# Layer 0 of a four-layer graph network: a prebuilt mark list, a last evaluation that only counts, shorter candidate lists, and a tie removal behind a branch

## The chip, the cores and the metric

The kernel runs on one NeuronCore of a Trainium2 chip. The core has five engines that run their own instruction streams in order and wait for each other through semaphores: TensorE (PE: matrix products and transposes into PSUM), VectorE (DVE), ScalarE (ACT), GpSimd (POOL, which here starts the indirect gathers) and SyncE (SP, which here starts nearly all other transfers). The metric is the time of one execution in microseconds (us) on the device. The kernel before took 3152.24 us (median of 3 runs, 3150.27 to 3155.07).

## The reference

The input is x (4096 nodes, 256 features) and adj (4096 x 4096, about one entry in a thousand nonzero, and a full diagonal). Four layers follow each other, each as `x = x + layer(relu(layernorm(x)), adj)`. Only layer 0 matters here:

```python
def _top_p_attention(X, W1, W2, W3):
    q = X @ W1.T @ W2.T
    k = X @ W3.T
    probs = softmax(q @ k.T / TAU)
    idx = jnp.argsort(-probs, axis=-1)
    sp = jnp.take_along_axis(probs, idx, axis=-1)
    cs = jnp.cumsum(sp, axis=-1)
    keep_sorted = cs - sp < TOP_P                     # TOP_P = 0.9
    mask = zeros(probs.shape, bool).at[rows, idx].set(keep_sorted)
    A = probs * mask
    return A / jnp.maximum(A.sum(-1, keepdims=True), 1e-12)

R = S + eye(N); R = R / R.sum(-1, keepdims=True)      # S is adj
Z = 0; Xf = X; Xa = X
for n in range(2):
    A = _top_p_attention(Xa, W1, W2, W3)
    Xf = R @ Xf
    Xa = A @ Xa
    Z = Z + Xf @ U1[n].T + Xa @ U2[n].T
h = X + Z
return layernorm(h) * ln_g + ln_b
```

So each of two steps needs, in every row of a 4096 x 4096 matrix of probabilities, the smallest set of largest entries whose sum reaches 0.9, and the product of that cut matrix with a 4096 x 256 one. No sort is needed: a threshold per row is enough, if it is the exact one and ties at it are treated as the sort treats them.

## The kernel before, in words

Rows are worked on in 32 blocks of 128. `layer0_step(n, ...)` builds step n. It is a software pipeline: one call of `period(b, ...)` issues parts of several blocks, in an order that is written out as text in `ORDERS[n]` (L1096). A word such as `take4@-1` calls `take`, group 4, for block b-1; `s1@2` calls the Sign evaluation 1 for block b+2. The order of the words is the order of the instructions on VectorE, ScalarE and TensorE, for these three are under a manual schedule; so a word that waits holds up all words behind it that use the same engine. `fill` words are places where a given number of steps of some other generator is issued (`period`, L1820, with the numbers in the loops near the end of the file).

What happens to one block, in order of time:

- `logits0/1` (L1139) multiply queries and keys on TensorE, `exps0/1` (L1158) take exponentials on ScalarE into the tile `e` (128 x 4096).
- Four evaluations look for a threshold. Words `s0 r0 s1 r1 s2 r2 s3 r3` are `evaluate` (L1170): with Sign, ScalarE counts the entries over the current guess, with Relu it sums what lies under it. 0 and 1 read 1024 columns, 2 and 3 all 4096. After evaluations 0, 1, 2 small 128 x 1 steps on VectorE (`measured`, `update`, `stepped`) make the next guess; the words are `first`, `second` (`second_short` in step 1) and `third`. After evaluation 3, `bound` (L1255) makes an upper end `hi` with a margin over the guess (constant `AHEAD`).
- `below` (L1328) takes the entries under `hi` into `near` (L1331, all 4096 columns); `maxima`, `some_maxima` list the eight largest of each of 16 segments (L1339); `order` merges them into a descending list of `LIST` = 48 per row, eight by eight (`listing`, L1350 MAX8 and L1353 MATCH_REPLACE8).
- `decide` (L1358) finds the exact threshold and the number of tied entries to leave out (`extra`); `cut` (L1401) zeroes everything under the threshold.
- `drop` removes the tied entries with one `match_replace` over 4096 columns (L1413). In step 0 it stands behind a branch: `ties_pe` (TensorE) sums `extra` over the rows, `ties` (ScalarE) casts that to an integer, and `tc.If` skips the removal where it is zero. In step 1 it always runs.
- `flip` g transposes four of the 32 128 x 128 pieces of `e` (TensorE, L1469), `take` g copies them to SBUF (ScalarE, L1475), `attend` g multiplies them with the node features (TensorE, L1484), g from 0 to 7; `attended` scales by the row sum's inverse (L1493).

Step 0 then does per block `turn` and `turned` (transposes), `keys` for step 1, and the products with U1 and U2: `xa_pe` and `h_pe` (`weighted`, L1519). `copy_xa` (ScalarE, L1542) copies one half of the result and `store_xa` (VectorE, L1546) adds the node's own features to the other half; `store_h` (L1536) copies the second product. Step 0 also marks where adj is nonzero: `load_adj` loads the 512 KB quarters of a block's rows, and eight `mark` words per period (L1498, 128 x 512 to 128 x 4 each) take the maxima of absolute values on VectorE. After step 0, `listed_columns` turns the marks into lists of columns (MAX8 and MATCH_REPLACE8 over 1024 columns, L794).

Step 1 uses the lists: `reach` (L1568) gathers the needed rows of adj and of node features with indirect transfers on POOL (`gather`, L835: 20 per period in the first half of the blocks, 10 gathers per block of nodes), and `mix` (L1581, products L850) forms R @ Xf from them. `mix0` and `mix1` work on two blocks per period; the first 16 periods make the first product, the second 16 the second one, and in the second half also the sum with the heads (`add_heads`, L1615), the layer norm (`spread`, `finish`, `level`, `normalised`) and the projection of layer 1. `verify` (L1444) tests in every row that the lists were long enough; if one was not, the whole layer is done again by a general and slow path (L2259).

Layers 1 to 3 follow and are not touched.

Of the kernel before, what the change touches and what calls it, by code (L numbers as in the profile page):

```python
# [63 lines left out]
F32 = mybir.dt.float32  # L64
# [6 lines left out]
ALU = mybir.AluOpType  # L71
# [5 lines left out]
P = 128  # L77
# [16 lines left out]
LIST = 48  # L94
AHEAD = 16.0
# [3 lines left out]
QUARTERS = 4  # L99
CHUNKS = 5  # L100
# [554 lines left out]
def fast_layers(  # L655
# [82 lines left out]
    def load_adj(pool, ib):  # L738

        parts = []  # L740
        for c in range(0, NB, CA):
            t = pool.tile([P, CA, P], F32, name="adj", tag="adj")
            nc.sync.dma_start(t, adjt[ib, :, c : c + CA, :])
            parts.append(t)
        return parts
# [282 lines left out]
    def front(h0, kt, xs):  # L1028
# [27 lines left out]
        for i in range(NB + LAG + 4):  # L1056
            o = i - LAG
            if i < NB:
# [3 lines left out]
                if i % 4 == 3:  # L1062
                    group = slice(i - 3, i + 1)
                    var = sm.tile([P, 4], F32, name="var4")
                    nc.vector.tensor_scalar_add(var, spread_[:, group, 1], LN_EPS)
                    nc.gpsimd.tensor_tensor(scale[:, group, 0], var, minus_half[:, :4], op=ALU.pow)
            if 0 <= o + 1 < NB:
                relu(o + 1)
# [30 lines left out]
    second attend4@-1 take6@-1 attend5@-1 mark s2@2 mark maxima fill flip7@-1 attend6@-1 take7@-1 r2@2 attend7@-1  # L1099
    order early logits0@3 attended@-1 mark turn_pe@-1 third fill turn@-1 exps0@3 keys_pe@-1 ties_pe logits1@3 cut  # L1100
    keys@-1 ties exps1@3 xa_pe@-1 s0@3 mark r0@3 drop copy_xa@-1 s3@2 store_xa@-1 flip0 mark flip1 mark
    take0 h_pe@-1 take1 fill first r3@2 flip2 attend0 mark mark attend1 store_h@-1 take2 flip3 take3 fill
# [4 lines left out]
    exps1@3 stood@-3 cut mix0 s0@3 laid@-3 s3@2 projected@-3 finish@-1 level@-2 mixed0 drop mix1 tabled@-3  # L1107
    r0@3 r3@2 attend7@-1 shifted@-2 fill first flip0 spread0 flip1 take0 heads@-1 other1 s1@3 attend0 take1 r1@3 flip2 flip3
# [17 lines left out]
    def layer0_step(n, va, kt, own, extra=None):  # L1126
# [43 lines left out]
        def evaluate(b, k, funcs=(AF.Sign, AF.Relu)):  # L1170
# [3 lines left out]
            if AF.Sign in funcs:  # L1174
                s["signs"], s["gap"] = small("signs"), small("gap")
                s.setdefault("at", ones)
# [42 lines left out]

        def stepped(to, m, t):  # L1220
# [34 lines left out]
        def bound(b):  # L1255

            s = state[b]
            low, steep, goal = yield from measured(b, 3)
# [21 lines left out]
            nc.vector.tensor_scalar_add(square[:, 1:2], square[:, 1:2], 1e-4)  # L1280
            yield
            nc.vector.scalar_tensor_tensor(
                square[:, 0:1], power, 1e-4, square[:, 0:1], op0=ALU.mult, op1=ALU.add
# [25 lines left out]
            nc.vector.scalar_tensor_tensor(ahead, final, AHEAD, by, op0=ALU.mult, op1=ALU.mult)  # L1309
# [3 lines left out]
            nc.vector.tensor_scalar(ahead, ahead, inverse, 3.0, op0=ALU.mult, op1=ALU.min)  # L1313
# [29 lines left out]
        def listing(b):  # L1343
# [3 lines left out]
            listed = tops[:, b % 4, 1:]  # L1347
            for k in range(0, LIST, 8):
# [3 lines left out]
                if k + 8 < LIST:  # L1352
                    nc.vector.match_replace(rest, listed[:, k : k + 8], src, 0.0)  # L1353
                    yield

            nc.gpsimd.tensor_copy(least[:, b : b + 1], listed[:, LIST - 1 :])

        def decide(b):  # L1358

            s, col = state[b], slice(b, b + 1)  # L1360
            listed, hi, room = tops[:, b % 4, 1:], end["hi"][:, col], end["room"][:, col]
            nc.vector.tensor_sub(room, s["low"], s["full_goal"])
            yield
            ahead_of = wk.tile([P, LIST], F32, name="ahead_of")
            nc.vector.tensor_tensor_scan(
                ahead_of, tops[:, b % 4, :LIST], tops[:, b % 4, :LIST], 0.0, op0=ALU.add, op1=ALU.bypass
            )
            yield
            out_ = wk.tile([P, LIST], F32, name="out_")
            nc.vector.tensor_scalar(out_, ahead_of, room, None, op0=ALU.is_ge)  # L1370
            yield
            kept = wk.tile([P, LIST], F32, name="kept")
# [12 lines left out]
            if n:  # L1385
                dropped(b)
                yield

        def dropped(b):

            s, col = state[b], slice(b, b + 1)
            s["drop"] = small("drop", 8)
            nc.vector.tensor_scalar(
                s["drop"], eights, end["extra"][:, col], end["t"][:, col], op0=ALU.is_lt, op1=ALU.mult
            )
# [9 lines left out]
        def drop(b):  # L1405

            s = state[b]
            with ExitStack() as only:
                if not n:
                    tied = nc.vector.value_load(s["tied"][0:1, 0:1], min_val=0, max_val=P * LIST)  # L1410
                    only.enter_context(tc.If(tied != 0))
                    dropped(b)
                nc.vector.match_replace(s["e"][:, ::-1], s["drop"], s["e"][:, ::-1], 0.0)  # L1413

        def ties_pe(b):

            s = state[b]
            if b == 0:
# [76 lines left out]
        def mark(b):  # L1495
            for q in range(QUARTERS):
                for part in (slice(0, CA // 2), slice(CA // 2, CA)):
                    nc.vector.tensor_reduce(  # L1498
                        marks[:, part, q, b],
                        state[b]["adj"][q][:, part, :],  # L1500
                        AX.X,
                        ALU.max,
                        apply_absolute_value=True,
                    )
                    yield

# [12 lines left out]
        def weighted(b, v):  # L1519

            pu = ps1.tile([P, 2, D], F32, name="pu", tag="pr")
            for k in range(DC):
# [5 lines left out]
                    stop=(k == DC - 1),  # L1528
                )
            state[b]["pu"] = pu  # L1530
# [9 lines left out]
        def copy_xa(b):  # L1540
            t = state[b]["hu"] = own.tile([P, 2, D + 1], F32, name="hu", bufs=2)
            nc.scalar.copy(t[:, 0, :D], state[b]["pu"][:, 0, :])  # L1542

# [771 lines left out]
```

## Time and profile before

The profiled execution took 3154.33 us; its span (first to last instruction) is 3152.2 us, the mean granted TensorE clock 0.934.

| stretch of the span, us | what runs | PE busy | DVE busy | ACT busy | POOL busy | clock |
|---|---|---|---|---|---|---|
| 0 to 100 | layer norm, keys of step 0 | 70.1 | 36.3 | 31.9 | 10.7 | 0.89 to 1.00 |
| 100 to 160 | step 0, first periods | 31.7 | 24.7 | 39.2 | 0 | 0.66 |
| 160 to 1220 | step 0 | 885.9 | 989.6 | 927.5 | 15.8 | 0.98 |
| 1220 to 1300 | end of step 0, lists | 43.5 | 65.4 | 48.5 | 0 | 0.74 |
| 1300 to 1400 | step 1, first periods | 63.1 | 90.9 | 86.8 | 65.1 | 0.80 |
| 1400 to 2420 | step 1 | 903.5 | 935.3 | 821.4 | 689.6 | 0.96 |
| 2420 to 3152 | layers 1 to 3 | 526.5 | 413.7 | 287.6 | 493.3 | 0.83 to 0.97 |

An engine's busy time is the time in which it executes something; what is missing to the length of the stretch is waiting. A busy share under 1 in every engine means that they wait for each other in turn. In the fences below a row of the timeline is: start in us, duration in us, engine, source line, operation, output <- input, shapes, count, and in brackets the idle time before it and what ended it. A row of the waits is: who waited for whom, total us, times, longest. A row of the groups is: line, engine, operation, tiles and shapes, count | busy us, mean ns of one | idle us before them. A row of the stretches is: its limits, its length, the busy time of PE, PE's weight loads, DVE, ACT and POOL (with counts), the granted clock, the share of the DMA engines and GB/s. The step 0 periods, from one L1401 to the next, have a mean of 32.42 us, those of the first half of step 1 32.28, those of the second half 34.43.

### The profile page before, as it was taken

The page shows a single profiled execution, that of the slowest core. Times are in us where ns is not written, and L with a number is a line of the kernel's source. Part 1 is how long each engine was busy: PE and PEld are TensorE (multiplying, and loading weights), DVE is VectorE, ACT ScalarE, POOL GpSimd, SP SyncE. Part 2 cuts the span into 40 slices and gives each one's busy share as a digit, 9 for nine tenths or more (in the row PEclk, how much of TensorE's full clock was granted, in tenths as well). Part 3 has the DMA queues.
Part 4 walks back from the last instruction along what each step waited for, and adds up shares of the span by engine and source line. Part 5 has one row for each costly group of instructions (what it writes and reads, how often), then busy time and mean ns, then how long its engine had stood idle before and what let it go on. Part 6 is the DMA issues. An engine that isn't in the chain of part 4 may idle for free. (4 is left out here: it accounts for less than half of the span.)

```text
span 3152.2 us, 44347 instructions
## 1 busy us (share of the span) xinstructions
PE 2524.1 (80%) x12468; PEld 1893.4 (60%) x12468; DVE 2555.9 (81%) x9611; ACT 2242.7 (71%) x3436; POOL 1274.5 (40%) x1350
## 2 busy tenths in 40 slices
PE   6658888888888887398998988999876776888666
PEld 5336556565656665176767667677765554788444
DVE  3389999999999998899999999999982776899200
ACT  3589999999999953888888888998932123899100
POOL 1000000000000000278888846566654775775576
PEclk9779999999999999699999999999988998999888
DMA  3012232322223233034444433334333874554575
GB/s 125 9 48 88 78 98 77 96 81 84 88 76 98 78 111 98 29 111 126 126 125 126 124 106 107 104 97 127 109 94 95 266 212 136 150 157 123 177 210 163
DMA packets 213852, 357.05 MB, mean 113 GB/s; under 512 B 33879, under 2 KB 147036, under 8 KB 213596
## 3 DMA queue, kind: packets, MB, share of 16 engines
q1 hardware_dynamic: 169100, 237.74, 23.6%
q0 software_dynamic: 43520, 116.14, 13.6%
q8 instruction: 102, 1.67, 0.2%
q14 instruction: 154, 1.26, 0.1%
q10 hardware_dynamic: 976, 0.23, 0.0%
HBM read 290.85 MB, written 63.13 MB: 112 GB/s over the span
## 5 line engine op out<-in xcount | busy, mean ns | idle before, releaser
L1178 ACT ACTIVATE unread<-e,next_pair 128x4096 uint8<-128x4096 f32 (+1 forms) x384 | 1098.2, 2860 | 50.0 <-DVE next_pair L1229 45.3
L1484 PE MATMUL pa<-va,at 128*128 128x256 f32 x2048 | 498.7, 392 | 60.3 <-DVE t L1615 45.0
L1484 PE MATMUL pa<-h,at 128*128 128x256 f32 x2048 | 472.2, 381 | 17.5 <-ACT at L1475 17.5
L1484 PEld LDWEIGHTS pa<-va,at 128*128 128x128 f32 x2048 | 384.8, 195 | 142.4 <-ACT at L1475 61.0
L1341 POOL COPY eighth<-best 128x16 f32<-128x16 f32 x64 | 21.6, 337 | 1039.2 <-DVE best L1339 824.9
L1475 ACT COPY at<-pat 128x512 f32<-128x512 f32 x512 | 285.1, 583 | 197.8 <-PE pat L1469 192.7
L1484 PEld LDWEIGHTS pa<-h,at 128*128 128x128 f32 x2048 | 377.3, 190 | 69.3 <-ACT at L1475 24.4
L1339 DVE MAX8 best<-near 128x8 f32<-128x256 f32 x1024 | 404.5, 418 | 3.2
L1469 PE MATMUL pat<-ident,e 128*128 128x128 f32 x2048 | 291.7, 279 | 100.4 <-ACT at L1475 55.1
L1469 PEld LDWEIGHTS pat<-ident,e 128*128 128x128 f32 x2048 | 247.3, 144 | 185.9 <-ACT at L1475 79.3
L835 POOL DMA_INDIRECT vg<-v_d,column x320 | 306.1, 956 | 118.7 <-issue 90.6
L1148 PE MATMUL pl<-kt,qb 64*128 64x512 f32 x1024 | 279.2, 656 | 75.8 <-ACT e L1162 75.7
L1162 ACT ACTIVATE e<-pl,minus_guess 128x1024 f32<-128x1024 f32 x256 | 282.9, 1111 | 44.7 <-PE pl L1148 34.3
L850 PE MATMUL acc<-vg,ac 128*128 128x256 f32 x768 | 228.9, 445 | 93.1 <-DMA vg<-v_d,column 73.0
L1331 DVE SCALAR_TENSOR_TENSOR near<-e,end_hi 128x4096 f32<-128x4096 f32 x64 | 286.7, 4480 | 0.1
L1401 DVE SCALAR_TENSOR_TENSOR e<-e,end_t 128x4096 f32<-128x4096 f32 x64 | 286.6, 4478 | 0.0
L835 POOL DMA_INDIRECT vg<-far_d,column x160 | 250.4, 1565 | 60.2 <-issue 41.8
L835 POOL DMA_INDIRECT vg<-mixed_d,column x160 | 219.1, 1369 | 86.2 <-issue 44.6
L850 PEld LDWEIGHTS acc<-vg,ac 128*128 128x128 f32 x768 | 157.9, 220 | 158.6 <-DMA vg<-v_d,column 100.6
L850 PE MATMUL pr<-vg,ac 128*128 128x257 f32 (+1 forms) x768 | 197.5, 409 | 56.1 <-issue 33.8
L2141 PE MATMUL acc<-u,tabg 128*65 128x128 f32 x1536 | 194.5, 281 | 45.3 <-DVE u L2126 44.2
L850 PEld LDWEIGHTS pr<-vg,ac 128*128 128x128 f32 x768 | 150.4, 202 | 104.8 <-issue 39.5
(554 smaller groups left out, 4483.7 us busy)
## 6 DMA issues: line engine op xcount, KB each, us to landing
adj<-in_adjt SPq DMA_DIRECT2D x128, 512.0 KB
ac<-adjc_d SPq DMA_DIRECT2D x96, 384.0 KB
adjc_d<-ac SPq DMA_DIRECT2D x32, 384.0 KB
vg<-v_d SPq DMA_DIRECT2D x64, 128.0 KB
targets<-steep_d SPq DMA_DIRECT2D x32, 256.0 KB
vg<-v_d,column POOLq DMA_INDIRECT x320, 4.0
table_d<-tab SPq DMA_DIRECT2D x32, 132.0 KB
tabg<-table_d SPq DMA_DIRECT2D x32, 132.0 KB
```

The lines of the kernel that those rows point to most:

```text
L835: nc.gpsimd.indirect_dma_start(out, None, rows, bass.IndirectOffsetOnAxis(ap=index, axis=0))
L850: nc.tensor.matmul(acc, ac[:, k, :], v[:, k, :], start=(k == 0), stop=(k == CHUNKS and not own))
L1148: nc.tensor.matmul(pl[:, r, :], s["qb"][rows], kt[rows, j * 512 : (j + 1) * 512], start=True, stop=True,)
L1162: nc.scalar.activation(s["e"][:, j * 1024 : (j + 1) * 1024], pl.rearrange("p r c -> p (r c)"), AF.Exp, bias=minus_guess[:, b : b + 1], acc ...
L1178: nc.scalar.activation(unread[:, :width], s["e"][:, :width], func, bias=s["at"], scale=-1.0, accum_out=s["signs"] if func == AF.Sign else ...
L1331: nc.vector.scalar_tensor_tensor(near, s["e"], end["hi"][:, b : b + 1], s["e"], op0=ALU.is_lt, op1=ALU.mult, accum_out=s["low"])
L1339: nc.vector.max(best[:, k, :], near[:, k * (N // SEG) : (k + 1) * (N // SEG)])
L1401: nc.vector.scalar_tensor_tensor(s["e"], s["e"], last, s["e"], op0=ALU.is_ge, op1=ALU.mult, accum_out=s["held"])
L1469: nc.tensor.transpose(pt[:, k, :], s["e"][:, c * P : (c + 1) * P], ident)
L1475: nc.scalar.copy(at, s["pt", g])
L1484: nc.tensor.matmul(s["pa"], s["at", g][:, k, :], va[:, c, :D], start=(c == 0), stop=(c == NB - 1))
L2141: nc.tensor.matmul(s["acc"][:, h, :], s["tab"][:, k, h * (DK + 1) : (h + 1) * (DK + 1)], s["u"][:, k, h, :], start=(k == 0), stop=(k == CH ...
```

## The change

- Marks: one generator `marking` takes over loading and marking adj, a full quarter (128 x 1024) per instruction, through four buffers. 16 of its 128 instructions stand in the front part (every second turn from i = 10 on), 36 in the fills of the three periods before block 0, then three per period.
- The last evaluation is only counted: the word `r3` is gone, and `bound` calls `counted` in place of `measured(b, 3)`: seven small VectorE operations in place of three, that work the sum under the guess out of the two last counts. The margin is made from the last step taken too (`SPREAD`, two more small operations), `AHEAD` is 11 in place of 16.
- Lists: 32 per row in step 0 and 40 in step 1, in place of 48.
- `store_xa` is gone: TensorE adds the node's own features as a product with the identity, and `copy_xa` copies both halves. It moves ahead of `s0`; it stood behind `r0`.
- Step 1: the removal of ties stands behind a branch as in step 0, with `ties_pe` and `ties` in step 1 as well. `ties_pe` writes to a PSUM tile of the tag that `mix0` uses too. The order of step 1 is written anew: `attend7@-1` ahead of the cut, `heads` and `finish` and `level` behind `drop`, `flip0` ahead of `mix1`, `s3` behind `mixed0`.

```diff
-LIST = 48
-AHEAD = 16.0
+LISTS = (32, 40)
+LIST = max(LISTS)
+AHEAD = 11.0
+SPREAD = 0.5
...
+    def marking(pool, marks):
+        parts = []
+        for k in range(NB * QUARTERS):
+            while len(parts) < min(k + ADJ_BUFS, NB * QUARTERS):
+                b, q = divmod(len(parts), QUARTERS)
+                parts.append(pool.tile([P, CA, P], F32, name="adj"))
+                nc.sync.dma_start(parts[-1], adjt[b, :, q * CA : (q + 1) * CA, :])
+            b, q = divmod(k, QUARTERS)
+            nc.vector.tensor_reduce(
+                marks[:, :, q, b], parts[k], AX.X, ALU.max, apply_absolute_value=True
+            )
+            yield
...
+            if i >= 10 and i % 2 == 0:
+                some(marked, 1)
...
-    second attend4@-1 take6@-1 attend5@-1 mark s2@2 mark maxima fill flip7@-1 attend6@-1 take7@-1 r2@2 attend7@-1
-    order early logits0@3 attended@-1 mark turn_pe@-1 third fill turn@-1 exps0@3 keys_pe@-1 ties_pe logits1@3 cut
-    keys@-1 ties exps1@3 xa_pe@-1 s0@3 mark r0@3 drop copy_xa@-1 s3@2 store_xa@-1 flip0 mark flip1 mark
-    take0 h_pe@-1 take1 fill first r3@2 flip2 attend0 mark mark attend1 store_h@-1 take2 flip3 take3 fill
+    second attend4@-1 take6@-1 attend5@-1 mark s2@2 maxima fill flip7@-1 attend6@-1 take7@-1 r2@2 attend7@-1
+    order early logits0@3 attended@-1 turn_pe@-1 third fill turn@-1 exps0@3 keys_pe@-1 ties_pe logits1@3 cut
+    keys@-1 ties exps1@3 xa_pe@-1 copy_xa@-1 s0@3 r0@3 mark drop s3@2 flip0 flip1
+    take0 h_pe@-1 take1 fill first flip2 attend0 mark attend1 store_h@-1 take2 flip3 take3 fill
...
-    exps1@3 stood@-3 cut mix0 s0@3 laid@-3 s3@2 projected@-3 finish@-1 level@-2 mixed0 drop mix1 tabled@-3
-    r0@3 r3@2 attend7@-1 shifted@-2 fill first flip0 spread0 flip1 take0 heads@-1 other1 s1@3 attend0 take1 r1@3 flip2 flip3
+    exps1@3 attend7@-1 stood@-3 ties_pe cut ties mix0 s0@3 laid@-3 r0@3 projected@-3 drop flip0 heads@-1 finish@-1 level@-2
+    mixed0 s3@2 mix1 tabled@-3 flip1 shifted@-2 fill first spread0 take0 other1 s1@3 attend0 take1 r1@3 flip2 flip3
...
+        def counted(b):
+            s = state[b]
+            pair, before, goal = s["next"], s["before"], s["full_goal"]
...
+            nc.vector.tensor_add(mass, t, before[:, 0:1])
+            nc.vector.scalar_tensor_tensor(mass, s["signs"], s["signs2"], mass, op0=ALU.subtract, op1=ALU.mult)
+            nc.vector.tensor_scalar(twice, s["signs"], float(N), t, op0=ALU.add, op1=ALU.mult)
+            nc.vector.scalar_tensor_tensor(low, mass, 0.25, before[:, 1:2], op0=ALU.mult, op1=ALU.add)
+            nc.vector.scalar_tensor_tensor(low, goal, 0.1, low, op0=ALU.mult, op1=ALU.max)
+            nc.vector.scalar_tensor_tensor(gap, twice, 0.5, low, op0=ALU.mult, op1=ALU.subtract)
+            nc.vector.scalar_tensor_tensor(steep, gap, -0.33 / 0.465, twice, op0=ALU.mult, op1=ALU.add)
...
         def drop(b):
-            s = state[b]
-            with ExitStack() as only:
-                if not n:
-                    tied = nc.vector.value_load(s["tied"][0:1, 0:1], min_val=0, max_val=P * LIST)
-                    only.enter_context(tc.If(tied != 0))
-                    dropped(b)
-                nc.vector.match_replace(s["e"][:, ::-1], s["drop"], s["e"][:, ::-1], 0.0)
+            s, col = state[b], slice(b, b + 1)
+            tied = nc.vector.value_load(s["tied"][0:1, 0:1], min_val=0, max_val=P * LIST)
+            with tc.If(tied != 0):
+                ties = small("drop", 8)
+                nc.vector.tensor_scalar(ties, eights, end["extra"][:, col], end["t"][:, col], op0=ALU.is_lt, op1=ALU.mult)
+                nc.vector.match_replace(s["e"][:, ::-1], ties, s["e"][:, ::-1], 0.0)
+
         def ties_pe(b):
-            if b == 0:
+            if n or b == 0:
                 bank = ps1.tile([P, 512], F32, name="pties", tag="pr")
...
+            if v == 0:
+                nc.tensor.matmul(pu[:, 1, :], ident, va[:, b, :], start=False, stop=True)
...
         def copy_xa(b):
             t = state[b]["hu"] = own.tile([P, 2, D + 1], F32, name="hu", bufs=2)
-            nc.scalar.copy(t[:, 0, :D], state[b]["pu"][:, 0, :])
-
-        def store_xa(b):
-            rows, t = slice(b * P, (b + 1) * P), state[b]["hu"]
-            nc.vector.tensor_add(t[:, 1, :D], va[:, b, :], state[b]["pu"][:, 1, :])
+            nc.scalar.copy(t[:, :, :D], state[b]["pu"])
+            rows = slice(b * P, (b + 1) * P)
             nc.sync.dma_start(heads_d[rows, :], t[:, 0, :D])
             nc.sync.dma_start(base_d[rows, :], t[:, 1, :D])
...
+            early = {
+                -3: ((0, 2), (0, 2), (3, 2), (0, 2)),
+                -2: ((3, 4), (9, 4), (9, 4), (9, 4)),
+                -1: ((0, 3), (0, 3), (0, 3), (0, 3)),
+            }
             for b in range(-3, NB):
-                period(b, guesses, {-3: (0, 0, 3, 0), -2: (3, 9, 9, 9)}.get(b, (0, 0, 0, 0)))
+                period(b, (guesses, marked), early.get(b, ((0, 0),) * 4))
+            some(marked, NB * QUARTERS)
```

## The prediction

> **What bounds the kernel now.** I read four views: the busy time of three stretches of ten periods each (a period is the time from one block's `cut`, L1401, to the next), the longest waits in such a stretch, the rows of one period, and the costliest groups.
>
> ```profile
> core 0: us, PE busy (x) PEld busy (x) DVE busy (x) ACT busy (x) POOL busy (x), PEclk, DMA share, GB/s
> 614.00:938.20 324.20, 277.66 (x1340) 194.65 (x1340) 305.90 (x1219) 300.68 (x390) 4.56 (x30) 1.00 0.27 86
> 1480.00:1802.80 322.80, 289.85 (x1405) 224.52 (x1403) 315.73 (x1212) 283.62 (x323) 263.21 (x220) 0.98 0.43 125
> 1879.00:2223.30 344.30, 311.84 (x1485) 242.86 (x1484) 328.80 (x1297) 305.41 (x390) 212.59 (x226) 0.96 0.36 108
> ```
>
> Step 0 (first row, period 32.42 us) keeps VectorE busy 30.6 us per block, ScalarE 30.1, TensorE 27.8. The first half of step 1 (period 32.28) has VectorE at 31.6. The second half (period 34.43) has VectorE at 32.9 and TensorE at 31.2. VectorE looks like the bound in all three; the waits say that it isn't alone. Step 0:
>
> ```profile
> PE pat L1469 <- ACT at L1475: 17.3, 10, 1.7
> ...
> ACT at L1475 <- PE pat L1469: 12.6, 10, 1.3
> DVE hu L1546 <- ACT hu L1542: 11.2, 10, 1.2
> ```
>
> TensorE and ScalarE wait for each other in every block: a round (transpose, copy, product) whose length doesn't fall with either engine's load. ScalarE's rows, one period:
>
> ```profile
> 709.95 0.46 ACT L1493 ACTIVATE xa<-pa,ra 128x256 f32<-128x256 f32 x1
> ...
> 715.81 1.09 ACT L1162 ACTIVATE e<-pl,minus_guess 128x1024 f32<-128x1024 f32 x1
> ...
> 719.56 3.71 ACT L1178 ACTIVATE unread<-e,next_pair 128x4096 uint8<-128x4096 f32 x1
> ...
> 723.26 1.06 ACT L1475 COPY at<-pat 128x512 f32<-128x512 f32 x2
> 724.21 3.72 ACT L1178 ACTIVATE unread<-e,next_pair 128x4096 uint8<-128x4096 f32 x1
> ```
>
> The last row is r3, which the change removes. While it runs, TensorE does its flips and products for the two chunks just copied:
>
> ```profile
> 723.89 0.66 PE L1469 MATMUL pat<-ident,e 128*128 128x128 f32 x4 [1.73 <-ACT at L1475]
> 724.38 3.62 PE L1484 MATMUL pa<-h,at 128*128 128x256 f32 x16
> ```
>
> The same place in the first block, after a longer idle time:
>
> ```profile
> 204.65 1.11 PE L1469 MATMUL pat<-ident,e 128*128 128x128 f32 x4 [4.92 <-ACT at L1475]
> 205.56 4.54 PE L1484 MATMUL pa<-h,at 128*128 128x256 f32 x16
> ```
>
> After 4.92 us of idling the same work takes 1.4 us more: the granted clock is 0.65 in 204.6 to 208.6, against 1.00 in all of 614 to 938, where no idle time of TensorE is over 1.74 us.
>
> The first half of step 1 is bound by POOL: its gathers (L835) follow each other every 1.25 us without a longer gap, 20 per block, and two per block are stretched while VectorE runs L1331 or L1401:
>
> ```profile
> 1619.22 4.80 POOL L835 DMA_INDIRECT vg<-far_d,column  x1 [0.30 <-issue]
> ...
> 1625.80 0.94 POOL L835 DMA_INDIRECT ac<-in_adjt,adj_row  x1 [0.31 <-issue]
> ...
> 1632.04 4.29 POOL L835 DMA_INDIRECT vg<-far_d,column  x1 [0.30 <-issue]
> ```
>
> 18 x 1.25 + (4.80 + 0.30) + (4.29 + 0.30) = 32.2, the period. L1413's match_replace runs from 1623.80 to 1628.21, and the gathers in it keep 0.94 to 0.98.
>
> ```profile
> L1178 ACT ACTIVATE unread<-e,next_pair 128x4096 uint8<-128x4096 f32 x256 | 949.9, 3711 | 28.5 <-DVE next_pair L1229 26.1 <-DVE m L1301 0.3
> L1413 DVE MATCH_REPLACE8 e<-drop,e 128x4096 f32<-128x4096 f32 x32 | 141.1, 4408 | 0.0
> ```
>
> **The change part by part.** The profiled execution took 3154.33 us, 2.09 over the median 3152.24 (span 3152.2, the rest around it). The sum is made against 3154.33.
>
> Front, 0 to 100 us: 16 full marks on VectorE, and adj loads on SP's queue. No row has a full mark; bounds are 1.36 (two halves of 0.68) and 1.12 (a quarter of L1401's 4.48), the nearest row MAX8 over 128x1024, 1.22. I take 1.13 from one start to the next. 18 us go into 50 us of VectorE's idling in 20 to 100, but in order: 0 to +6, taken +1. SP's queue issues four loads ahead; at 291 GB/s in the first 20 us four tiles of 512 KB cost 7 us there if they push the front's own loads back, which is that +6.
>
> Ramp, 100 to 193: 36 marks (41 us) in three periods. VectorE is busy 24.7 of 60 us in 100 to 160, so they fit, but each fill puts two to four ahead of the small steps that ScalarE waits for, while ScalarE gains two r3 (7.6). Between 0 and +22 (half of the marks exposed); taken +11, the middle, for want of a nearer row.
>
> Step 0, per block. VectorE: eight half marks out (0.60 apart, -4.8), three full ones in (+3.4), two listing rounds out (MAX8 0.29, MATCH_REPLACE8 0.28, MATCH_VALUE_LOAD 0.09, 0.715 apart: -1.4), L1546 out (-0.3, and its 1.1 wait), six small operations in (0.15 each, +0.9): 30.6 to 28.3. ScalarE: r3 with its accumulator read out (-3.8), copy_xa twice as wide (0.59 for 0.35): 30.1 to 26.5. TensorE: +0.45 for the identity product of two instructions: 28.2. If load decided, the period would fall to about 31. I follow the round instead, from ScalarE's `attended` (T, 709.95 above):
> - exponentials end at T+6.95 (716.90), as now. copy_xa now waits here for xa_pe (TensorE ends at 717.29 now, +0.45): done T+8.25. s0, r0 behind it: T+10.66 (2.41). s3: T+14.36 (3.70). take0: flip2 can begin at T+14.99. Now it begins at T+13.94.
> - flip2, attend0, attend1, flip3 on TensorE: 3.9; take3 begins T+19.6. Nothing of r3 hides this any more. take3 (0.5), s1 and r1 (1.2 each) in order: T+22.5, against T+21.75 now (731.70).
> - update on VectorE (twelve small steps, 2.3) beside take4 to take6: s2 begins T+24.84. s2, take7, r2 (3.70 + 0.47 + 3.70): T+32.72.
>
> The same sum for the kernel before gives 32.55, 0.13 more than measured, so the round costs +0.17 per block: r3's 3.8 us become idle time. And TensorE, done with h_pe at about T+10.9 (two 1 us products behind copy_xa), idles 4.1 us before flip2, where it idled 1.73. By the rows after 3.5 to 6.4 us of idling, the slow stretch behind it costs 1.05 to 2.0 (1.05 at 204.65, 1.22 at 1341.02, 1.36 at 2378.05, 1.99 at 2308.26, from the distances between its matmuls), all on the round; taken 1.3. Together +1.5 x 28 = +42. Bounds: -1.4 (load decides) to +2.7 per block, -39 to +75.
>
> [...]
>
> Last two periods of step 0: -1. Close and listing: 0. Step 1's prologue has ScalarE at 87 of 100 us (1300 to 1400) and loses two r3 with half of them hidden: -3.5 (-8 to 0).
>
> Step 1, first half. match_replace leaves VectorE (-4.4), r3 ScalarE (-3.8); but POOL's chain is untouched: 0 per block (-1 to +1 on 16). The one POOL wait there, 6.8 us at 1357.75 for TensorE's mix, goes as the blocks before it come sooner: -7 (-7 to 0).
>
> [...]
>
> Step 1, second half, 15 periods. VectorE: -4.4 match_replace and its load -0.1, -0.3 dropped, -0.7 one listing round, +0.9 small operations, +0.3 value_load and branch (0.24 idle at step 0's branch at 1193.42): 32.9 to 28.6. ScalarE 30.5 - 3.8 + 0.14 (ties' cast) = 26.9. TensorE stays at 31.2, of which the slow stretch after its 2.29 us wait for add_heads (L1615, now straight after the cut) is about 1; without that wait some 30, plus 0.2 for ties_pe; mix0 then waits up to 0.5 for the cast, with everything behind it on TensorE. I take 30.7, TensorE's own work: -3.7 x 15 = -55 (-1.3 to -4.3 per block, -20 to -65). Branches on the other engines: no idle time at step 0's, taken 0. Ties are taken as rare enough that the removal is skipped; each block with one costs 5 us.
>
> Sum: 1 + 11 + 42 - 1 - 3.5 - 7 - 55 = -12.5: 3141.8 profiled, against the median 3139.
>
> **The rivals.**
> - A, the forecast, 3112 to 3150: step 0 loses by its round and clock, step 1's second half gains more. 0.42.
> - B, step 0 loses nothing: with no slow clock its term is +5 and the time 3102; if load decides, -39 and 3058. For it: ScalarE and VectorE get 3.5 and 2.3 us of room. Against: the waits above, and 204.65. 0.22.
> - C, the other side: the slow stretch costs 2.0 per block (2308.26) and 0.3 the round: +64, 3161. It decides from +1.95 per block on, since the other terms sum to -54.5. For it: the round may idle TensorE at a second place too; against: the nearest gap, 4.92, cost 1.05. 0.26.
> - D, the second half shrinks only by the heads' wait, 1.3: TensorE's 31.2 hold and mix0's wait for the cast takes the rest: -20, 3174. 0.10.
>
> **How the numbers follow.** A measurement tells about 0.2% (6 us) from no change. Faster: A but 0.05, and B: 0.59. Same: 0.05 of A and 0.04 of C: 0.09. Slower: the rest of C, and D: 0.32. The range 3085 to 3180 leaves out B's lower part and the tails of C and D, under 0.2 together; A's own is 3112 to 3150.
>
> **What would show it.** Right: step 0's cut-to-cut 33.5 to 34.5, TensorE idle about 4 us before flip2 with ScalarE's take0 as the releaser, granted clock there below 0.97; POOL's gathers still without gaps up to the middle of step 1 at 32.2 per block; the second half at 30 to 31.5 with no TensorE wait for add_heads. Wrong: a step 0 period under 32.4 (then VectorE's relief counts), a first half off 32.2, or a new TensorE wait for `tied` over 1 us.

## The result and the profile after

The changed kernel takes 3191.8 us (median of 4 runs, 3191.3 to 3195.6) against 3151.6 of the kernel before: 1.3% slower, ratio 1.0129 with a 95% interval of 1.0111 to 1.0146. The forecast was 3139 with a range of 3085 to 3180. The profiled span went from 3152.2 to 3189.1 us. Cut by the starts of `cut` (numbered 0 to 31 in step 0 and 32 to 63 in step 1), the 36.9 us lie as follows (the ramp is the three periods before block 0, the close the last parts of step 0, the prologue step 1 up to its first cut):

| stretch | before | after | difference | forecast |
|---|---|---|---|---|
| start to cut 0 (front, ramp) | 193.4 | 211.4 | +18.0 | +12 |
| cut 0 to 29 (step 0) | 941.0 | 1005.2 | +64.2 | +42 |
| cut 29 to 31 | 53.7 | 44.7 | -9.0 | -1 |
| cut 31 to 32 (close, lists, prologue) | 138.3 | 143.1 | +4.8 | -3.5 |
| cut 32 to 48 (step 1, first half) | 518.4 | 510.9 | -7.5 | -7 |
| cut 48 to 63 (second half) | 516.6 | 493.6 | -23.0 | -55 |
| cut 63 to the end | 790.8 | 780.2 | -10.6 | 0 |

In the changed kernel the lines have moved: `evaluate` is L1190, `flip` L1507, `take` L1513, `attend` L1522, `copy_xa` L1570, the marks L750, `cut` L1438, `shifted` L1684, the gathers L843. Busy time in just under ten periods of step 0, in a stretch of step 1's first half and in ten periods of its second half (columns as in the stretches before):

```profile
core 0: us, PE busy (x) PEld busy (x) DVE busy (x) ACT busy (x) POOL busy (x), PEclk, DMA share, GB/s
626.10:971.60 345.50, 293.64 (x1356) 211.48 (x1356) 282.80 (x1147) 268.68 (x369) 4.55 (x30) 0.94 0.22 65
1500.00:1860.00 360.00, 323.32 (x1568) 251.43 (x1566) 294.61 (x1332) 276.26 (x344) 293.32 (x247) 0.95 0.44 125
2008.80:2350.10 341.30, 307.77 (x1522) 239.48 (x1521) 281.28 (x1311) 269.94 (x384) 207.64 (x230) 0.99 0.38 109
```

Per block of step 0, VectorE fell from 30.6 to 28.4 us and ScalarE from 30.1 to 27.0, close to the 28.3 and 26.5 worked out, and yet the period rose from 32.4 to 34.7. No engine is near full any more. The waits in step 0 say who waits:

```profile
PE pat L1507 <- ACT at L1513: 45.1, 10, 4.5
...
ACT at L1513 <- PE pat L1507: 57.4, 27, 5.9
```

Both stood at 1.7 and 1.3 us per block before; now TensorE waits 4.5 for ScalarE's copies, and after that ScalarE up to 5.9 for TensorE's transposes. One period of ScalarE:

```profile
763.03 0.47 ACT L1531 ACTIVATE xa<-pa,ra 128x256 f32<-128x256 f32 x1
...
770.88 0.59 ACT L1570 COPY hu<-pu 128x512 f32<-128x512 f32 x1 [0.76 <-PE pu L1557]
...
777.62 1.06 ACT L1513 COPY at<-pat 128x512 f32<-128x512 f32 x2
...
784.56 0.58 ACT L1513 COPY at<-pat 128x512 f32<-128x512 f32 x1 [4.92 <-PE pat L1507]
...
797.63 0.47 ACT L1531 ACTIVATE xa<-pa,ra 128x256 f32<-128x256 f32 x1
```

and of TensorE in the middle of it:

```profile
778.23 0.75 PE L1507 MATMUL pat<-ident,e 128*128 128x128 f32 x4 [4.50 <-ACT at L1513]
778.78 5.26 PE L1522 MATMUL pa<-h,at 128*128 128x256 f32 x16
783.87 0.60 PE L1507 MATMUL pat<-ident,e 128*128 128x128 f32 x4
```

The sixteen products took 3.62 us before the change and take 5.26 here, after 4.50 us of idling: the slow clock (granted clock 0.57 from 778.2 to 782.2 us). r3's place on ScalarE, 3.8 us, is now an idle 4.92.

In the ramp, VectorE puts four marks (4.59 us) in a row ahead of steps that ScalarE waits for:

```profile
133.01 4.59 DVE L750 TENSOR_REDUCE marks<-adj 128x8 f32<-128x1024 f32 x4
...
142.86 4.59 DVE L750 TENSOR_REDUCE marks<-adj 128x8 f32<-128x1024 f32 x4
...
157.27 1.15 ACT L1190 ACTIVATE unread<-e,next_pair 128x1024 uint8<-128x1024 f32 x1 [9.34 <-DVE next_pair L1271]
```

Some of them wait themselves: from 100 to 211 us VectorE idles 6.7 us ahead of seven marks until their quarter of adj has landed.

In step 1's second half, a wait that was small before stands out (rows of VectorE, GpSimd and ScalarE):

```profile
2158.39 0.16 DVE L1684 SCALAR_TENSOR_TENSOR shift<-two,scale 128x2 f32<-128x2 f32 x1 [4.92 <-POOL scale L1678]
...
2151.37 1.09 POOL L1657 TENSOR_TENSOR scale<-var,minus_half 128x1 f32<-128x1 f32 x2 [7.59 <-DVE var L1655]
...
2157.66 0.70 POOL L1678 TENSOR_TENSOR scale<-two,minus_half 128x2 f32<-128x2 f32 x1
...
2160.80 1.15 ACT L1190 ACTIVATE unread<-e,next_pair 128x1024 uint8<-128x1024 f32 x1 [3.36 <-DVE next_pair L1271]
```

The same place in the kernel before:

```profile
2020.70 4.41 DVE L1413 MATCH_REPLACE8 e<-drop,e 128x4096 f32<-128x4096 f32 x1
...
2025.86 0.16 DVE L1659 SCALAR_TENSOR_TENSOR shift<-two,scale 128x2 f32<-128x2 f32 x1 [0.76 <-POOL scale L1653]
...
2018.83 1.09 POOL L1632 TENSOR_TENSOR scale<-var,minus_half 128x1 f32<-128x1 f32 x2 [6.96 <-DVE var L1630]
...
2025.13 0.70 POOL L1653 TENSOR_TENSOR scale<-two,minus_half 128x2 f32<-128x2 f32 x1
```

GpSimd's 7 us of `finish` and `level` ran beside match_replace (2020.70 to 2025.11), and `shifted` waited 0.76 us. Without match_replace VectorE arrives 4 us sooner and waits them: 4.92. Over ten periods of each kernel, before and after:

```profile
DVE shift L1659 <- POOL scale L1653: 5.6, 8, 0.8
DVE shift L1684 <- POOL scale L1678: 49.3, 10, 5.1
```

`first` is written behind `shifted`, and s1, `second_short` and s2 behind `first`. The removed work had been the cover of another engine's chain.

Of the runs below, both_marks_in_waits, first_ahead_of_finish, lists_48, both_marks_again, copy_xa_between and copy_xa_between_again were made on chips on which the kernel before itself took 3403 to 3425 us; in the profiles taken there step 1 and the later layers are longer by something that the profile doesn't name (680 to 693 us from cut 32 to 48, where the other runs have 510 to 518); from these only step 0, which is as long there as elsewhere, and ratios to the kernel before on the same chip are used.

### The profile page after: what moved, and what is told of

It reads as the page before. It is cut to its first block, busy times and chain, and to the rows that moved or that the text cites. A ratio compares the mean times of both kernels' runs of the same rounds, so it can differ in the third digit from the quotient of the medians.

```text
span 3189.1 us, 44419 instructions
## 1 busy us (share of the span) xinstructions
PE 2556.5 (80%) x12596; PEld 1933.7 (61%) x12596; DVE 2370.4 (74%) x9451; ACT 2024.9 (63%) x3340; POOL 1271.6 (40%) x1350
## 3 DMA queue, kind: packets, MB, share of 16 engines
q8 instruction: 103, 1.69, 0.2%
## 5 line engine op out<-in xcount | busy, mean ns | idle before, releaser
L1190 ACT ACTIVATE unread<-e,next_pair 128x4096 uint8<-128x4096 f32 (+1 forms) x320 | 859.5, 2686 | 142.5 <-DVE next_pair L1271 112.8
L1522 PE MATMUL pa<-h,at 128*128 128x256 f32 x2048 | 512.1, 405 | 0.0
L1522 PE MATMUL pa<-va,at 128*128 128x256 f32 x2048 | 486.5, 386 | 13.8 <-ACT at L1513 13.8
L1513 ACT COPY at<-pat 128x512 f32<-128x512 f32 x512 | 287.1, 579 | 298.4 <-PE pat L1507 293.6
L1522 PEld LDWEIGHTS pa<-h,at 128*128 128x128 f32 x2048 | 410.5, 207 | 57.0
L1522 PEld LDWEIGHTS pa<-va,at 128*128 128x128 f32 x2048 | 377.0, 192 | 104.4 <-ACT at L1513 33.3
L1507 PE MATMUL pat<-ident,e 128*128 128x128 f32 x2048 | 305.2, 283 | 162.3 <-ACT at L1513 155.1
L1507 PEld LDWEIGHTS pat<-ident,e 128*128 128x128 f32 x2048 | 252.2, 145 | 235.2 <-ACT at L1513 182.1
L843 POOL DMA_INDIRECT vg<-v_d,column x320 | 306.1, 957 | 117.7 <-issue 89.3
L1438 DVE SCALAR_TENSOR_TENSOR e<-e,end_t 128x4096 f32<-128x4096 f32 x64 | 286.6, 4478 | 0.0
L843 POOL DMA_INDIRECT ac<-in_adjt,adj_row x160 | 229.0, 1431 | 48.1 <-issue 37.7
L843 POOL DMA_INDIRECT vg<-mixed_d,column x160 | 205.2, 1282 | 68.7 <-issue 44.6
L843 POOL DMA_INDIRECT vg<-far_d,column x160 | 187.3, 1170 | 59.7 <-issue 46.6
```

The costliest lines, as they stand in the source:

```text
L843: nc.gpsimd.indirect_dma_start(out, None, rows, bass.IndirectOffsetOnAxis(ap=index, axis=0))
L1190: nc.scalar.activation(unread[:, :width], s["e"][:, :width], func, bias=s["at"], scale=-1.0, accum_out=s["signs"] if func == AF.Sign else ...
L1438: nc.vector.scalar_tensor_tensor(s["e"], s["e"], last, s["e"], op0=ALU.is_ge, op1=ALU.mult, accum_out=s["held"])
L1507: nc.tensor.transpose(pt[:, k, :], s["e"][:, c * P : (c + 1) * P], ident)
L1513: nc.scalar.copy(at, s["pt", g])
L1522: nc.tensor.matmul(s["pa"], s["at", g][:, k, :], va[:, c, :D], start=(c == 0), stop=(c == NB - 1))
```

## The experiments

Unless said otherwise an edit is made to the changed kernel (3191.8 us; step 0 34.67 per period, second half of step 1 33.94, the length that most of its periods have). Most edits were measured once; where one kernel was run four to nine times on one of these chips, its times lie within 4 to 8 us.

### Step 0: the place of s3

```diff
-    keys@-1 ties exps1@3 xa_pe@-1 copy_xa@-1 s0@3 r0@3 mark drop s3@2 flip0 flip1
-    take0 h_pe@-1 take1 fill first flip2 ...
+    keys@-1 ties exps1@3 xa_pe@-1 copy_xa@-1 s0@3 r0@3 mark drop flip0 flip1
+    take0 h_pe@-1 take1 s3@2 fill first flip2 ...
```

> The changed kernel with one word moved in step 0's order: s3 stands behind take1 (where r3 stood before the change) instead of ahead of flip0. Theory (round and clock): take0 and take1 then run as soon as flip0 and flip1 are done, TensorE does flip2, attend0, attend1 and flip3 beside s3's 3.7 us, its 4.5 us gap ahead of flip2 goes and with it the slow clock (granted clock back to 0.99 or 1.00 in step 0). Step 0's period falls from 34.67 us to 30.5 to 31.5, the time from 3192 to about 3085 to 3105. Rival (VectorE's full marks, their loads, or the identity product and the wider copy make the loss): the period stays within 1 us of 34.67, the time over 3160.

Measured: 3089.7 us, period 31.4, and in the stretch 600 to 900 us the clock is whole:

```profile
600.00:900.00 300.00, 269.58 (x1300) 189.35 (x1300) 271.56 (x1136) 254.04 (x349) 4.56 (x30) 1.00 0.22 71
```

One word was worth 102 us. The marks, the identity product and the wide copy are all still in it, so they are not what made step 0 slow; the order of s3 and take0 is. The kept traces say the same of the marks: in the changed kernel the last of them is at 1066.6 us and the periods behind it are as long as those ahead (34.2 to 35.9). Only with s3 moved do the marks count: there the period falls from 31.4 to 30.3 us when they have run out (984.8 us).

### Step 0: the clock alone

```diff
-            for k in range(DC):
+            for k in [i % DC for i in range(DC * (3 if v else 1))]:
                 nc.tensor.matmul(
...
```

> The changed kernel with the products of h_pe issued three times in step 0 (the same result, 3.8 us of additional TensorE work per block in the gap ahead of flip2). Theory: the gap shrinks from 4.5 to under 1 us, the granted clock in step 0 returns to 1.00, and the period falls by the slow stretch's 1.6 us to about 33.0, although TensorE has more to do: time about 3146. Rival (the clock has no part in it, only the order of waits): period unchanged at 34.6 or longer, time 3190 or more.

Measured: 3152.6 us. The period is 32.9 in every block, TensorE's gap 1.08 us, and the clock is whole (first the wait ahead of flip2, nine blocks, then the stretch 600 to 900 us):

```profile
PE pat L1507 <- ACT at L1513: 9.7, 9, 1.1
...
600.00:900.00 300.00, 283.57 (x1315) 194.72 (x1315) 259.60 (x1071) 245.57 (x337) 4.56 (x30) 1.00 0.22 68
```

More work for TensorE made each block 1.75 us faster: that much of the 2.25 us that the changed kernel loses per block is the slow stretch. The time came out 6 us over the expected one, since the additional products cost 9 us in the close.

### Step 0: the place of copy_xa

```diff
-    ... xa_pe@-1 copy_xa@-1 s0@3 r0@3 mark drop s3@2 flip0 flip1
+    ... xa_pe@-1 s0@3 r0@3 copy_xa@-1 mark drop s3@2 flip0 flip1
```

> The changed kernel with copy_xa moved back behind r0 in step 0's order. Theory (round and clock): s0 no longer waits for the products of xa_pe, s3 begins about 0.8 us sooner, h_pe on TensorE ends about 2 us later and its gap ahead of flip2 is 2 to 3.5 us; so 0.8 of the round's 0.6 comes back, and the slow stretch stays in most blocks: period 33.0 to 34.0, time 3145 to 3175. Rival (the place of copy_xa is the whole cause of step 0's loss): period back to 32.4, time about 3125.

Measured: 3139.0 us, better than the range given; mean period 32.73. The gap ahead of flip2 is 2.19 us. Of 28 blocks, twelve show no slow stretch (period 31.6 to 31.9) and sixteen one that costs 1.68 us from flip2 to flip3 (period 33.3 to 33.6). So the place of copy_xa is worth more than the round's sum gave: 1.3 us of waiting (34.67 less 1.8 for the mean slow stretch, less 31.6) and a gap behind which the clock stayed whole in twelve of 28 blocks (it was 0.97 from 600 to 900 us). Both explanations have a part; the numbers fit neither alone.

### Step 0: r3 put back

```diff
-                s["gap"] = small("gap") if k < 3 else None
+                s["gap"] = small("gap")
-    take0 h_pe@-1 take1 fill first flip2 ...
+    take0 h_pe@-1 take1 fill first r3@2 flip2 ...
```

> The changed kernel with r3 issued again in step 0, at its place in the kernel before (its sum is written but not used). Theory (round and clock): ScalarE idles 4.9 us between the copies of take2 and take3, and r3's 3.8 us fit into that, so step 0's period stays within 0.3 us of the changed kernel's 34.7 and the time within 10 us of 3192. Rival (ScalarE's load counts in step 0): the period rises by 2 to 3.8 us, the time to 3250 or more.

Measured: 3193.8 us, period 34.70. The whole removed evaluation, 3.8 us per block on ScalarE, was worth nothing in this order.

### The marks ahead of block 0

```diff
-                -3: ((0, 2), (0, 2), (3, 2), (0, 2)),
-                -2: ((3, 4), (9, 4), (9, 4), (9, 4)),
-                -1: ((0, 3), (0, 3), (0, 3), (0, 3)),
+                -3: ((0, 0), (0, 0), (3, 0), (0, 0)),
+                -2: ((3, 0), (9, 0), (9, 0), (9, 0)),
+                -1: ((0, 0), (0, 0), (0, 0), (0, 0)),
-    ... flip2 attend0 mark attend1 store_h@-1 ...
+    ... flip2 attend0 mark attend1 mark store_h@-1 ...
```

> The changed kernel without the 36 marks in the three periods before block 0; four instead of three marks per period from block 0 on. Theory (marks stand ahead of the small steps that ScalarE waits for in these periods): the first cut comes at 195 to 200 us instead of 211.4, step 0's period is unchanged at 34.7 since VectorE idles there, the time 3192 - 12 to - 17. Rival (the first periods are late for another reason, and a fourth mark costs its 1.2 us per block): first cut still at 208 or later, or a period of 35.9.

Measured: 3166.5 us; the first cut comes at 185.7, earlier than expected and 7.7 us earlier than in the kernel before (two r3 of 3.8 are gone there; that these are the 7.7 was not tested). The 36 marks had cost 25.7 us, not 12 to 17 (between all the runs with them, 207.9 to 213.1, and all without, 185.5 to 188.6, it is 23 in the mean); the fourth mark per period cost nothing in step 0 (1005.2 us from cut 0 to 29 in both).

### Step 1: the place of shifted

```diff
-    below second_short ...
+    below shifted@-3 second_short ...
-    ... mix1 tabled@-3 flip1 shifted@-2 fill first ...
+    ... mix1 tabled@-3 flip1 fill first ...
```

The order behind the last block gets the same word, behind `opened`.

> The changed kernel with one word moved in step 1's order: shifted stands behind the next period's below instead of ahead of first. Theory (VectorE waits 4.9 us per period in step 1's second half for GpSimd's chain of finish and level, and first, s1, second_short, s2 and r2 stand behind that wait): the wait falls under 0.5 us since below's 4.5 us cover it, the second half's period falls from 33.94 to 30.7 to 31.5, the time by 35 to 48 us to about 3145 to 3157. Rival (the second half is held by mix0's wait for the cast of tied, or by TensorE's own load): the wait moves, the period stays over 33. Step 0 is as in the changed kernel by both.

Measured: 3169.9 us; the second half's period is 31.85, the wait for GpSimd gone. That is 22 us of the expected 35 to 48; from cut 48 to 63 it takes 472.5 us, 44.1 less than the kernel before, against the -55 forecast. Part of the rest is seen in VectorE's rows, here with GpSimd's below them:

```profile
2148.13 0.77 DVE L1473 SCALAR_TENSOR_TENSOR ra<-end_extra,end_t,held 128x1 f32<-128x1 f32 x1
2148.82 0.20 DVE L1220 TENSOR_SCALAR twice<-signs,ones 128x1 f32<-128x1 f32 x1
2148.95 0.15 DVE L1477 RECIPROCAL ra<-ra 128x1 f32<-128x1 f32 x1
...
2150.89 0.76 DVE L1285 SCALAR_TENSOR_TENSOR step_num<-pair,end_goal,gap 128x1 f32<-128x1 f32 x1
...
2148.16 1.41 POOL L1660 TENSOR_TENSOR h<-h,g_all 128x256 f32<-128x256 f32 x2
...
2150.91 1.40 POOL L1662 TENSOR_TENSOR h<-h,xb 128x256 f32<-128x256 f32 x2
```

`first` now runs beside `finish`, and its steps with two tensor inputs take 0.45 to 0.77 us in place of 0.15 to 0.22; those with one input stay at 0.14 to 0.20. It costs 2.8 us per period.

### Step 1: a shorter finish

```diff
-            nc.gpsimd.tensor_mul(y, y, g_all)
-            nc.gpsimd.tensor_add(y, y, b_all)
             nc.gpsimd.tensor_add(y, y, s["xb"])
```

> The changed kernel, in its own order, with the multiplication by the layer norm's gain and the addition of its offset left out of finish (two of the five GpSimd operations on 128x256, 1.4 us each). Theory (first waits behind shifted for the end of GpSimd's chain): VectorE's wait of 4.9 us falls to about 2.1, the second half's period from 33.9 to about 31.2, the time by 28 to 40 us to 3152 to 3164. Rival (TensorE's or ScalarE's waits set the period): under 8 us less.

Measured: 3153.2 us; the second half's period is 31.2, and VectorE's wait

```profile
DVE shift L1682 <- POOL scale L1676: 19.8, 9, 2.4
```

is 2.2 us in the mean where it was 4.9. 2.7 us of GpSimd's chain are 2.7 us of the period: the chain is the bound of that half.

### Step 1: match_replace in every block

```diff
-            tied = nc.vector.value_load(s["tied"][0:1, 0:1], min_val=0, max_val=P * LIST)
-            with tc.If(tied != 0):
+            with ExitStack() as only:
+                if not n:
+                    tied = nc.vector.value_load(s["tied"][0:1, 0:1], min_val=0, max_val=P * LIST)
+                    only.enter_context(tc.If(tied != 0))
```

> The changed kernel with step 1's match_replace out of its branch, in all 32 blocks. Theory (POOL's gathers bound the first half of step 1, VectorE's path to GpSimd's finish the second): the first half, cut 0 to cut 16, stays within 5 us of 511; in the second half the 4.4 us stand ahead of heads, finish and the wait for GpSimd, so each period grows by about 4.4 to some 38, +60 in all: time about 3245 to 3260. Rival (VectorE's load counts in the first half as well): +4.4 for each of 31 blocks, first half over 560, time over 3310.

Measured: 3253.3 us. The first half takes 512.1 us from cut 32 to 48 (510.9 without): nothing. The second half's period is 38.3, +4.4. In the changed kernel's order match_replace no longer lies beside `finish` but ahead of it.

### Both moves, and the lists

`s3_and_shift` has the two edits of s3 and shifted together.

> The changed kernel with both words moved: s3 behind take1 in step 0, shifted behind the next period's below in step 1. If the two causes are independent the gains add: 3191.8 - 102 - 22 = 3068, ratio to the kernel before 0.973. If one of them only uncovers the other's stage (step 1 waits for something of step 0), less than 100 is gained.

Measured: 3073.6 us, ratio to the kernel before 0.975 (0.9734 to 0.9766). The gains add; this kernel beats both.

`lists_48_again` sets its LISTS back to (48, 48).

> The kernel of s3_and_shift with lists of 48 in both steps: two rounds of 0.72 us more per block in step 0, one in step 1. If the round of TensorE and ScalarE is the bound in step 0: its period stays at 31.3; if VectorE's chain from cut to cut is the bound in the second half of step 1: +0.7 per period there, +10 in all, about 3084. If VectorE's load decides everywhere: +50, about 3124.

Measured: 3084.6 us. Step 0 stays (905.1 us from cut 0 to 29 against 905.4), the second half of step 1 is 8 us longer, its first half 5. The shorter lists are worth about 11 us, all of it in step 1. The first run of it (lists_48) showed the same in step 0.

### Finish behind first

```diff
-    ... projected@-3 drop flip0 heads@-1 finish@-1 level@-2
-    mixed0 s3@2 mix1 tabled@-3 flip1 fill first spread0 ...
+    ... projected@-3 drop flip0
+    mixed0 s3@2 mix1 tabled@-3 flip1 fill first heads@-1 finish@-1 level@-2 spread0 ...
```

(from `s3_and_shift`, with shifted behind `maxima`)

> The kernel of s3_and_shift with heads, finish and level behind first in step 1, and shifted behind maxima. Theory (two-input steps on VectorE are stretched beside GpSimd's two-input operations): first's steps take 0.15 to 0.21 us, the second half's period falls from 31.9 to 30 to 31, the time by 12 to 25 us against 3073.6. Rival: period 31.5 or more.

Measured: 3085.6 us, slower than `s3_and_shift`; the second half's period is 33.7 in the mean of ten. `first` was back at 0.15 to 0.22 us (one step 0.26), as expected, but the price only moved. GpSimd now does its gathers first and `finish` behind them, beside the two-input steps of `bound`:

```profile
2130.83 4.60 DVE L1313 TENSOR_TENSOR total<-next_pair 128x2 f32<-128x2 f32 x1
...
2131.24 1.40 POOL L1660 TENSOR_TENSOR h<-h,g_all 128x256 f32<-128x256 f32 x2
...
2133.99 1.40 POOL L1662 TENSOR_TENSOR h<-h,xb 128x256 f32<-128x256 f32 x2
```

An addition of 128x2 elements, 0.15 us in the changed kernel (2167.19), takes 4.60 us and ends (2135.43) when the last of GpSimd's operations on h ends (2135.39). The expected 30 to 31 us were wrong; that VectorE's step is stretched beside GpSimd's is plain in these rows.

### The kernels with all moves

`all_moved` adds the marks from block 0 on to the kernel above, the fourth of a period beside the third ahead of drop.

> The changed kernel with four moves: s3 behind take1 and no marks ahead of block 0 but four per period (step 0), heads, finish and level behind first and shifted behind maxima (step 1). If the causes found are independent, from s3_and_shift's 3073.6: -26 to -22 for the marks, -12 to -25 for the second half: 3027 to 3040, ratio to the kernel before 0.960 to 0.965.

Measured: 3069.9 us, ratio 0.9734 (0.9721 to 0.9748), 30 us over the range: the marks' gain is there (first cut at 188.6), the loss of the moved finish too. `both_marks_again` has the marks moved with `finish` left where `s3_and_shift` has it; `copy_xa_between` moves copy_xa between s0 and r0 as well.

> The kernel of s3_and_shift without the 36 marks ahead of block 0, the fourth mark of each period beside the third ahead of drop. Theory: first cut at 187 to 189 us instead of 213, step 0's 29 periods 909 instead of 905, the rest unchanged: 3073.6 - 22 = 3048 to 3056, ratio to the kernel before 0.967 to 0.970.

> The same, with copy_xa between s0 and r0. If ScalarE's wait of 1.0 us for the products of xa_pe lies on the way that sets step 0's period: up to -1 per block, -10 to -28. If that period is set by VectorE's chain from r0 to s2 (ScalarE waits 1.8 us for VectorE ahead of s2): within 5 us of both_marks_again.

> The changed kernel with s3 behind take1, copy_xa between s0 and r0, four marks per period and none ahead of block 0, shifted behind below. From s3_and_shift's 3073.6: -24.5 (first cut at 188.5 instead of 213.1) and 880.5 - 905.4 = -25 in step 0: 3024, between 3015 and 3040; ratio to the kernel before 0.957 to 0.965. Where the kernel before takes 3420 us or more: ratio 0.985 to 0.988, as last time.

Measured: both_marks_again 3403.2 us, ratio 0.9928 (0.9911 to 0.9945), with the first cut at 187.3 and 909.3 us from cut 0 to 29, as expected; the ratio is not the expected 0.967 to 0.970, on a chip where the kernel before takes 3424.6 (the first run of it, both_marks_in_waits: 187.1 and 909.3). copy_xa_between takes 880.5 us there, a full 1.0 us less per block, so ScalarE's wait for the products of xa_pe does lie on the way: 3377.3 us, ratio 0.9859 (0.9839 to 0.9879). A second measurement: 3353.5, ratio 0.9860 (0.9842 to 0.9877). What it takes where the kernel before takes 3152 us was not measured; from `s3_and_shift` less 24 and 25 us it would be an estimated 3025.

## Why the prediction was wrong, point by point

Between the forecast's -12.5 us and the measured +36.9 lie 49 us: 32 in step 1's second half and 22 in step 0; the other terms come to -5 together.

**Step 0's mechanism: right.** The period did not follow the engines' loads; r3's time turned into idling, TensorE idled before flip2, and the clock fell behind the gap. r3_back, h_pe_thrice and s3_behind_take1 show the three parts. **Its size: the term +1.5 x 28 was mis-sized; it measured +2.2 x 29.** Against the offsets of the forecast (from `attended`): flip2 begins at T+15.2 (14.99), take3 at T+21.5 (19.6 + 1.3 = 20.9), the next `attended` at T+34.6 (32.72 + 1.3 = 34.0). In the mean over 24 blocks the slow stretch costs 1.8 us (from flip2 to flip3, less the 3.95 us that this takes at full clock), where I took 1.3. That figure was read too low from its own rows: taken from the first matmul behind the gap, the four of the prediction cost 1.33 (204.65), 1.50 (1341.02), 1.68 (2378.05) and 2.54 (2308.26), mean 1.76, against 1.05, 1.22, 1.36 and 1.99 there; and of nine gaps of 2.3 us in the kernel before, from 1994 to 2270 us, six are followed by a slow stretch that costs 1.61 to 1.69. The other 0.45 of the 2.25 is the round, where I had 0.17: the 0.13 that I took off for the hand's error should have stayed on, and some 0.15 of small steps are missing. That the gap grows was read right, why it had been short was read half: before, h_pe waited 0.50 us for `store_xa` on VectorE and so ended 1.73 us before flip2. Of the 2.77 us by which the gap grew, 1.5 are h_pe ending sooner after `attended`, the rest is flip2 beginning later.

**The slow stretch: rightly taken in every block.** In the changed kernel it follows the 4.5 us gap in all 24 blocks looked at (granted clock 0.50 from 778.70 to 782.00 us, 1.00 from 776.0 to 778.6 and from 782.2 to 785.0), with costs that repeat every six blocks (1.69, 1.64, 1.43, 1.33, 2.96, 1.69). The clock's falls and the blocks keep different steps: the granted clock falls at 778.67, 812.80, 846.94, 881.07 and 915.20 us, each 34.13 us after the last (the next, at 952.75, 37.55 us), while the blocks follow each other every 34.2 to 35.9. After the 2.19 us gaps of copy_xa_behind_r0 there is a slow stretch in sixteen of 28 blocks, after the gaps of 1.64 to 1.74 us in step 0 of the kernel before in none of 28 (granted clock 1.00 from 225 to 1130 us). What sets the sixteen apart from the twelve is not shown here.

**The ramp: +11 was mis-sized.** It measured +18 with the front. Without the marks it would be -7.7, so the marks cost 25.7 us, 0.7 us of each mark's 1.2; I had capped their exposure at half, and had not asked whether their loads would be there in time (6.7 us of waiting for them).

**Step 1's first half: right.** POOL's gathers hold it: 32.3 us per period in the mean of two, though now in turns of 30.3 and 34.4. -7.5 us against -7, and POOL's one wait of 6.8 us is gone. Taking match_replace away or putting it back moves nothing there (510.9 and 512.1 us).

**Step 1's second half: the step that failed.** "I take 30.7, TensorE's own work: -3.7 x 15 = -55": it measured 33.9 and -23.0, of which 13 come from the last two periods and 7 from the first three, and 2.9 from the ten in between. Not TensorE's work set the period but VectorE's wait of 4.9 us for GpSimd's chain of `finish` and `level`. I subtracted match_replace from VectorE's load and never asked what ran beside it. The order text shows it: `finish` and `level` moved behind `drop`, with `shifted` and `first` close behind, and no word was left between them that takes VectorE's time. The 0.76 us wait for `scale` in the kernel before was the row to read: a wait that small at the end of a 7 us chain means that something covers the chain. shift_behind_below and finish_shorter show that this wait was the bound; match_replace_always shows that in the new order match_replace would not have covered it either.

**The rivals.** C's condition (1.95 us per block) was met with 2.2, and D's outcome (the second half hardly shrinks) came too, by another mechanism than the one I gave it: mix0's wait for the cast of `tied` is 0.2 us. Each alone was in the range (3161 and 3174); together they make 3196 by the forecast's own terms, outside, and 3192 was measured. The range took the cases one at a time although nothing ties them.

**Small terms.** The last two periods of step 0 gave 9 us instead of 1, the close and the prologue came out 8 above the forecast, and the stretch from the last cut on gave 10.6 that I had at nothing. match_replace_always has 6.8 of these 10.6 back in its one run, so they are probably mostly the last block's match_replace. That these terms took some 10 us off the miss is luck. The prologue's share wasn't tested.

## What to carry to other kernels

Before crediting removed work, look at what runs beside it on the other engines: if a wait that follows it is nearly zero, the removed time can turn into that wait, and it takes a new order (here one word moved) to be worth anything. Where two engines hand tiles back and forth, put the long operation of the one behind the copies that the other waits for, not ahead of them; and don't count an idle gap on TensorE as free: here 1.3 to 3 us more came behind each gap of 4.5 us, 1.68 us behind sixteen of 28 gaps of 2.19 us, nothing behind those of 1.64 to 1.74 us. Independent bad cases add, so a range has to hold their sum.

## What the runs showed of the hardware beside that

VectorE's small operations with two input tiles took longer beside GpSimd's TENSOR_TENSOR on 128x256: the same 128x1 steps took 0.15 to 0.26 us without it (first_ahead_again) and 0.45 to 0.77 beside it (shift_behind_below), and one 128x2 addition took 4.60 us beside three pairs of them in place of 0.15 (first_ahead_again, and the changed kernel). One-input steps took 0.14 to 0.20 us beside it, and match_replace 4.41 us (2020.70 in the kernel before) as in the mean of its 32 blocks. The 4.60 us span six of GpSimd's instructions (1.4 us per pair), the 0.45 to 0.77 us about one; what makes this difference is not shown.
